# A graph-attention kernel: edge weights read from PSUM, and gathers issued in pairs behind VectorE's instructions

## The chip, the cores and the metric

The kernel runs on one core of a Trainium2 chip. The metric is the time of one execution in microseconds of the device (us). The core has TensorE (PE in the profile), VectorE (DVE), ScalarE (ACT), GpSimd (POOL) and SyncE (SP, which here only issues DMAs). They run side by side, each through its own list of instructions in order, and wait for each other by semaphores. PSUM is the memory TensorE writes to; it is divided into banks of 512 fp32 numbers per partition.

## What is computed

One layer of graph attention over 12,500 nodes of 256 features and 200,000 edges sorted by their target node `dst`:

```
h = relu(layernorm(x))
q, k, v = h @ Wq, h @ Wk, h @ Wv            # 8 heads of 32
logits = sum_d(q[dst] * k[src]) / sqrt(32)  # per edge and head
expv = exp(logits - segment_max(logits, dst)[dst])
agg = segment_sum(expv / segment_sum(expv, dst)[dst] * v[src], dst)
h2 = gelu(agg + h @ Wskip)
out = x + layernorm(h + h2)
```

Biases, gamma and beta are in the reference too.

## The kernel before

A first stage (to about 383 us) computes h, q, k and v for all nodes, writes them to tables in device memory (k and v together as 512 fp32 numbers a node, `kv_tab`), and plans the walk over the edges.

The walk (`walk_streams`) cuts the sorted edges into 8 streams of 25,000 edges and goes through all of them at once in 66 steps of 3 tiles (the last has 2). In a tile, each of 128 partitions holds one edge of each stream. Tile j of step c goes through these functions:

- `gather` (L1008): 8 indirect DMAs on POOL, one per stream, each fetching 128 rows of `kv_tab` into a quarter-megabyte slice of a buffer `kv`. There are 6 such buffers, so tile j of step c+2 takes the buffer of tile j of step c. `gather_next` (L1016) calls it right after the weighing that frees the buffer; all 8 are then in POOL's list.
- `spread` (L1042): TensorE multiplies a one-hot matrix with a window of q, which gives q of each edge's target in PSUM (`ps_qe`).
- `times` (L1054), twice per tile (streams 0 to 3 and 4 to 7): VectorE multiplies `ps_qe` with k, in place in `kv`.
- `total` (L1061): VectorE sums over the 32 numbers of a head: the logits L.
- `turn` (L1070): TensorE transposes L into PSUM (`ps_x`), edges along the free dimension. With tile 0, ScalarE then copies the last maximum of the step before into column 0 (L1077).

Once all 3 tiles of a step are turned, `maxima` (L1080) runs two scans and a subtraction on VectorE, `exponent` the exponential on ScalarE, `turn_back` (L1095) three transpositions on TensorE back to edges on partitions, in `ps_x`, and `weights` (L1104) a ScalarE copy from there to `w` in SBUF. `carried` (L1111) copies the weights of tiles 1 and 2 into `vw`. `weigh` (L1120) multiplies, on VectorE, the weights (each broadcast over 32 numbers) with v from `kv` into `vw` (L1124), and for tile 0 also L1129. `add_up` then sums `vw` over the edges of a node with TensorE, by one-hot matrices.

`ps_x` is a new tile of one bank in each step, from a pool with one buffer.

Beside the walk, nodes whose sums are complete are finished in pairs of 128-node blocks (`Pair`, L810), one stage a step: first `turn`, `divisors`, `divide`, `skip` (8 matmuls, L864), `add` (VectorE, L869) and `gelu`, in the next step `stats` (L875 and after), `root` (ScalarE, with a table load), `factors`, `scale` (L892, L896) and `store`. Pairs begin at step 10; not every step has one.

The order of each engine's work is written out by hand: `keep` (L779) ties each instruction to the one before it on the same engine. VectorE's order in the main loop, for step c, is: `times(c, 2)` twice, `total(c, 2)`, `weigh(c-1, 2)`, `maxima(c)`, `stats`, `times(c+1, 0)` twice, `total(c+1, 0)`, `weigh(c, 0)`, `divisors`, `divide`, `factors`, `add`, `times(c+1, 1)` twice, `total(c+1, 1)`, `weigh(c, 1)`, `scale`. TensorE's has `spread`, `turn`, the sums, `hot_n` and `hot_e` (one-hot matrices) and a pair's `turn` and `skip` between them.

The functions that the change touches, with the line numbers of the profile:

Of the kernel before, what the change touches and what calls it, by code (L numbers as in the profile page):

```python
# [28 lines left out]
F32 = mybir.dt.float32  # L29
# [5 lines left out]
OP = mybir.AluOpType  # L35
AX = mybir.AxisListType
SP = mybir.EngineType.SP
PSUM = bass.MemoryType.PSUM
DRAM = bass.MemoryType.DRAM

P = 128
HEADS = 8
# [4 lines left out]
S = 8  # L47
K = 3
# [712 lines left out]
def walk_streams(tc, N, HID, NST, KL, many, ident, idx, d0_row, slot_row, near, near_n, e_tab, pen_tab, h_tab,  # L761
# [174 lines left out]
    with ExitStack() as es:  # L936
# [35 lines left out]
        def tiles_of(c):  # L972
            return KL if c == NST - 1 else K


        step = [dict() for _ in range(NST + 3)]

        def where(s):
# [26 lines left out]
                q = at_byte(q_b, node, w // 2, KV).rearrange("n (k d) -> (n k) d", k=2)  # L1005
                keep(nc.sync.dma_start(qw[at:at + w, i, :].bitcast(U8), q))

        def gather(c, j):  # L1008
            t = gath.tile([P, S, KV], F32, name="kv")
            for s in range(S):  # L1010
                nc.gpsimd.indirect_dma_start(  # L1011
                    out=t[:, s, :], out_offset=None, in_=kv_tab[:, :],
                    in_offset=bass.IndirectOffsetOnAxis(ap=idx[:, s, j, c:c + 1], axis=0))
            step[c].setdefault("kv", []).append(t)

        def gather_next(c, j):  # L1016

            if c + 2 < NST and j < tiles_of(c + 2):
                gather(c + 2, j)

        def hot_e(c, i):

# [31 lines left out]
        def times(c, j, half):  # L1054

            g = step[c]
            k = g["kv"][j][:, 4 * half:4 * half + 4, :HID].rearrange("p (a b) d -> p a b d", a=2)
            keep(nc.vector.tensor_tensor(k, g["qe", half].rearrange("p b a d -> p a b d"), k,  # L1058
                                         op=OP.mult))

        def total(c, j):  # L1061
            g = step[c]
            if j == 0:
                g["L"] = work.tile([P, K, SH], F32, name="L")
            keep(nc.vector.tensor_reduce(g["L"][:, j, :].rearrange("p (s h) -> p s h", s=S),  # L1065
                                         g["kv"][j][:, :, :HID].rearrange(
                                             "p s (h d) -> p s h d", h=HEADS),
                                         AX.X, OP.add))

        def turn(c, j):  # L1070

            g = step[c]
            if j == 0:
                g["xt"] = xt_ps.tile([P, 512], F32, name="ps_x")
            keep(nc.tensor.transpose(g["xt"][:SH, j * P:(j + 1) * P], g["L"][:, j, :], ident))  # L1075
            if j == 0:
                keep(nc.scalar.copy(g["xt"][:SH, 0:1],  # L1077
                                    low0 if c == 0 else step[c - 1]["M"][:, CH - 1:]))

        def maxima(c):  # L1080
            g = step[c]
            n = tiles_of(c) * P
            X, R, pen = g["xt"][:SH, :n], g["xt"][SH:, :n], g["pen"]
            M = g["M"] = work.tile([SH, CH], F32, name="M")[:, :n]
            W = g["W"] = work.tile([SH, CH], F32, name="W", bufs=1)[:, :n]
            keep(nc.vector.tensor_tensor_scan(R, pen[:SH, :n], X, -BIG, op0=OP.add, op1=OP.max))  # L1086
            keep(nc.vector.tensor_tensor_scan(mirrored(M, 0, n), mirrored(pen[SH:, :], 1, n),  # L1087
                                              mirrored(R, 0, n), -BIG, op0=OP.add, op1=OP.max))
            keep(nc.vector.tensor_tensor(W, X, M, op=OP.subtract))

        def exponent(c):
            W = step[c]["W"]
            keep(nc.scalar.activation(W, W, AF.Exp))

        def turn_back(c):  # L1095
            g = step[c]

            n = tiles_of(c)
            ps = g["xt"][:, :K * SH].rearrange("p (k n) -> p k n", k=K)
            for j in range(n):  # L1100
                keep(nc.tensor.transpose(ps[:, j, :], g["W"][:, j * P:(j + 1) * P],
                                         ident[:SH, :SH]))

        def weights(c):  # L1104
            g = step[c]
            n = tiles_of(c)
            ps = g["xt"][:, :K * SH].rearrange("p (k n) -> p k n", k=K)
            g["w"] = work.tile([P, K, SH], F32, name="w", bufs=1)
            keep(nc.scalar.copy(g["w"][:, :n, :], ps[:, :n, :]))  # L1109

        def carried(c):  # L1111

            g = step[c]
            g["vw"] = [work.tile([P, S, SUMS], F32, name="vw", bufs=K) for _ in range(K)]
            keep(nc.scalar.copy(wden[c % 2][0:1], g["kv"][0][0:1, :, HID - HEADS:HID]))
            for j in range(1, tiles_of(c)):
                keep(nc.scalar.copy(g["vw"][j][:, :, :HEADS],
                                    g["w"][:, j, :].rearrange("p (s h) -> p s h", s=S)))

        def weigh(c, j):  # L1120
            g = step[c]
            t = g["vw"][j]
            wj = g["w"][:, j, :].rearrange("p (s h) -> p s h", s=S)
            keep(nc.vector.tensor_tensor(  # L1124
                t[:, :, HEADS:].rearrange("p s (h d) -> p s h d", h=HEADS),
                wj[:, :, :, None].to_broadcast([P, S, HEADS, D]),
                g["kv"][j][:, :, HID:].rearrange("p s (h d) -> p s h d", h=HEADS), op=OP.mult))
            if j == 0:
                keep(nc.vector.tensor_tensor(t[:, :, :HEADS], wj, wden[c % 2], op=OP.mult))  # L1129
# [100 lines left out]
        for c in range(NST - 1):  # L1230
# [9 lines left out]
                windows(c + 2)  # L1240
            for half in range(2):
                times(c, K - 1, half)
                spread(c + 1, 0, half)
            total(c, K - 1)
            turn(c, K - 1)
            if c:
                weigh(c - 1, K - 1)
                gather_next(c - 1, K - 1)
            maxima(c)
            if before:  # L1250
                before.stats()
            if c:
# [3 lines left out]
            turn_back(c)  # L1256
            if c:
                add_up_results(c - 1, 1)
            weights(c)
# [82 lines left out]
            pair.divisors()  # L1342
            pair.divide()
        turn_back(c)
        weights(c)
        carried(c)
        if before:
            before.root()
# [406 lines left out]
```

## Time and profile before

| | |
|---|---|
| three runs | 2769.89, 2772.73, 2779.48 us (median 2772.73) |
| the profiled execution | 2777.54 us; its span, from the first to the last instruction, 2775.8 us |
| busy, share of the span | DVE 74%, POOL 73%, PE 61%, ACT 38% |
| gathers (L1011) | 1576, 1827.4 us busy, from 383.7 to 2688.8 us |
| weighing (L1124) | 197 instructions, 449.7 us |
| `times` (L1058) | 394 instructions, 475.8 us |
| DMA share of 16 engines | 0.75 from 432 to 816 us, 0.80 from 816 to 2690 us |

A row of groups in the profile reads: line, engine, operation, output<-input, count | busy us, mean ns of one | idle time of the engine just before them, and what ended most of it. A row of the timeline reads: start, duration, engine, line, operation, output<-input, count, and in brackets the idle time before it and who ended it; where there is no bracket there was none. "issue" is idle time in which the engine waited for nothing that the profile shows. A gather's row shows POOL's part, the making of the transfer's descriptors; the transfer itself runs on the DMA engines after that.

### The profile page before, as it was taken

The numbers are of one execution on the slowest core, as the hardware profiler recorded it, in microseconds if no ns is written. First come the engines' busy times: TensorE is split into PE (matmuls) and PEld (weight loads), VectorE is DVE, ScalarE is ACT, GpSimd is POOL, SyncE is SP. The second block draws the span as 40 slices with busy tenths as digits, with TensorE's granted clock in tenths as the row PEclk, the third lists the DMA queues.
The fourth block names the chain that finished last, engine by engine and source line by source line (L and its number), as shares of the span: only waits on it lengthen the run. The fifth ranks groups of instructions, "written<-read, shape, count | busy, mean of one in ns | idle before, by whom it ended". The sixth has DMA issues, their size and how long they took to land.

```text
span 2775.8 us, 28386 instructions
## 1 busy us (share of the span) xinstructions
PE 1689.7 (61%) x7374; PEld 860.0 (31%) x7374; DVE 2048.7 (74%) x2416; ACT 1059.1 (38%) x2425; POOL 2028.5 (73%) x1767
## 2 busy tenths in 40 slices
PE   6779864444456656656565656566566556566554
PEld 3445432222223323322232333233233223233222
DVE  8766936666667777777777877777778778777674
ACT  3333322222234434444434434444444344344343
POOL 5634657777777777777777777777777777777760
PEclk9999975555566656566555655565666566565556
DMA  8667777777777887887788788787878878878853
GB/s 294 243 248 282 272 258 225 223 219 221 219 241 223 251 249 239 249 254 235 236 246 247 239 248 247 239 245 241 250 234 245 248 231 245 259 224 250 256 173 95
DMA packets 309574, 662.25 MB, mean 239 GB/s; under 512 B 53217, under 2 KB 193000, under 8 KB 304404
## 3 DMA queue, kind: packets, MB, share of 16 engines
q0 software_dynamic: 128768, 423.23, 50.8%
q1 hardware_dynamic: 179746, 236.30, 25.4%
q8 instruction: 61, 1.00, 0.2%
q14 instruction: 113, 0.93, 0.1%
q10 hardware_dynamic: 886, 0.79, 0.1%
HBM read 539.04 MB, written 121.07 MB: 238 GB/s over the span
## 4 chain that ended last, share of the span: by engine, by line
POOL 40%; DMA 16%; issue 16%; DVE 15%; PE 9%; ACT 2%; SPq 0%; DVEq 0%; another core or an unknown queue 0%; POOLq 0%; ACTq 0%
POOL kv L1011 39%; DMA kv<-kv_tab,idx 13%; DVE kv L1058 4%; PE ps_kv L258 4%; DVE vw L1124 3%; DVE L L1065 2%; PE ps_q L264 2%; PE ps_a L864 2%; DMA out_dram<-sums 1%; DVE M L1087 1%; DVE ps_x L1086 1%; DVE st L879 1%; ACT L885 1%; DMA sums<-table 0%; DVE sums L875 0%
## 5 line engine op out<-in xcount | busy, mean ns | idle before, releaser
L1011 POOL DMA_INDIRECT kv<-kv_tab,idx x1576 | 1827.4, 1160 | 482.2 <-issue 446.3
L1058 DVE TENSOR_TENSOR kv<-ps_qe,kv 128x1024 f32<-128x1024 f32 x394 | 475.8, 1219 | 442.9 <-DMA kv<-kv_tab,idx 433.6
L1049 PE MATMUL ps_qe<-qw,to_e 64*128 64x256 f32 (+1 forms) x1576 | 343.7, 416 | 542.2 <-DVE kv L1058 538.7
L1049 PEld LDWEIGHTS ps_qe<-qw,to_e 64*128 64x128 f32 (+1 forms) x1576 | 239.9, 265 | 760.1 <-DVE kv L1058 717.6
L1124 DVE TENSOR_TENSOR vw<-w,kv 128x2048 f32<-128x2048 f32 x197 | 449.7, 2283 | 10.7 <-ACT w L1109 10.7
L1065 DVE TENSOR_REDUCE L<-kv 128x64 f32<-128x2048 f32 x197 | 450.4, 2286 | 6.9 <-DVE kv L1058 0.2
L1148 PE MATMUL ps_a<-vw,to_n 128*32 128x264 f32 (+1 forms) x2344 | 318.1, 579 | 119.6 <-DVE vw L1124 117.2
L1028 ACT ACTIVATE to_e<-ps_hot,ones 128x384 fp32r<-128x384 f32 x396 | 213.3, 578 | 402.6 <-PE ps_hot L1026 392.7
L1160 ACT COPY sums_w<-ps_a 128x264 f32<-128x264 f32 x130 | 49.3, 380 | 804.7 <-PE ps_a L1148 552.0
L258 PE MATMUL ps_kv<-w_kv,hT 128*128 128x512 f32 x392 | 200.4, 633 | 23.2 <-ACT hT L141 22.0
L1026 PE MATMUL ps_hot<-et,near 48*128 48x384 bf16 x396 | 156.3, 457 | 67.2 <-ACT to_e L1028 62.2
L864 PE MATMUL ps_a<-w_s,hT 128*128 128x256 f32 x368 | 168.0, 636 | 44.8 <-ACT hT L850 43.4
L1148 PEld LDWEIGHTS ps_a<-vw,to_n 128*32 128x32 f32 (+1 forms) x2344 | 108.8, 155 | 279.1 <-DVE vw L1124 153.4
L270 POOL TENSOR_TENSOR qp<-qp 128x256 fp32r<-128x256 f32 x98 | 90.1, 921 | 139.0 <-ACT qp L269 138.7
L1148 PE MATMUL ps_hot<-vw,to_n 128*64 128x264 f32 x808 | 190.1, 639 | 0.0
L1075 PE MATMUL ps_x<-ident,L 128*64 128x128 f32 x197 | 78.0, 396 | 169.3 <-DVE L L1065 168.9
L1039 ACT ACTIVATE to_n<-ps_hot,ones 128x384 f32<-128x384 f32 x197 | 105.1, 579 | 124.6 <-PE ps_hot L1037 120.1
L1166 ACT COPY kv<-ps_a 1x264 f32<-1x264 f32 x388 | 143.2, 369 | 6.4
L864 PEld LDWEIGHTS ps_a<-w_s,hT 128*128 128x128 f32 x368 | 113.9, 324 | 89.2 <-ACT hT L850 64.7
L970 ACT ACT_TABLE_LOAD x102 | 130.9, 1283 | 1.9
L869 DVE TENSOR_TENSOR sums<-ps_a,sums 128x512 f32<-128x512 f32 x46 | 31.8, 691 | 134.6 <-PE ps_a L864 134.6
L264 PE MATMUL ps_q<-w_q,hT 128*128 128x256 f32 x392 | 106.4, 395 | 36.7 <-DVE qp L268 36.7
(267 smaller groups left out, 1925.6 us busy)
## 6 DMA issues: line engine op xcount, KB each, us to landing
qw<-q_pc SPq DMA_DIRECT2D x264, 128.0 KB
kv<-kv_tab,idx POOLq DMA_INDIRECT x1576
kv_tab<-kvo SPq DMA_DIRECT2D x16, 1280.0 KB
q_pc<-qp SPq DMA_DIRECT2D x16, 1280.0 KB
qw<-q_pc SPq DMA_DIRECT2D x264, 64.0 KB
table<-sums_w SPq DMA_DIRECT2D x264, 61.9 KB
pen<-pen_tab SPq DMA_DIRECT2D x66, 192.5 KB
sums<-table SPq DMA_DIRECT2D x92, 132.0 KB
```

What stands on the lines that cost most here:

```text
L258: ins = nc.tensor.matmul(ps_kv, hT[:, c, :], w_kv[:, c, :], start=c == 0, stop=c == KC - 1)
L264: ins = nc.tensor.matmul(ps_q, hT[:, c, :], w_q[:, c, :], start=c == 0, stop=c == KC - 1)
L864: self.keep(nc.tensor.matmul(self.ps[:, b, :], self.hT[:, b, c, :], w_s[:, c, :], start=False, stop=c == KC - 1, skip_group_check=True))
L1011: nc.gpsimd.indirect_dma_start(out=t[:, s, :], out_offset=None, in_=kv_tab[:, :], in_offset=bass.IndirectOffsetOnAxis(ap=idx[:, s, j, c:c ...
L1026: keep(nc.tensor.matmul(ps[:, :CH], near[:, i * P:(i + 1) * P], step[c]["et"], start=True, stop=True))
L1028: keep(nc.scalar.activation(step[c]["to_e"][:, i, :], ps[:, :CH], AF.Relu, scale=-1.0, bias=ones))
L1049: keep(nc.tensor.matmul(ps[:, b, a, :], g["to_e"][at:at + w, i, j * P:(j + 1) * P], g["qw"][at:at + w, i, :], start=True, stop=True))
L1058: keep(nc.vector.tensor_tensor(k, g["qe", half].rearrange("p b a d -> p a b d"), k, op=OP.mult))
L1065: keep(nc.vector.tensor_reduce(g["L"][:, j, :].rearrange("p (s h) -> p s h", s=S), g["kv"][j][:, :, :HID].rearrange("p s (h d) -> p s h d" ...
L1124: keep(nc.vector.tensor_tensor(t[:, :, HEADS:].rearrange("p s (h d) -> p s h d", h=HEADS), wj[:, :, :, None].to_broadcast([P, S, HEADS, D] ...
L1148: keep(nc.tensor.matmul(ps[at:at + w, :], g["to_n"][:, j, i * P + at:i * P + at + w], g["vw"][j][:, s, :], start=j == 0, stop=j == tiles_o ...
L1166: keep(nc.scalar.copy(step[c + 1]["kv"][0][0:1, s, HID - HEADS:], ps[at:at + 1, :]))
```

## The change

`ps_x` becomes one tile for the whole walk, `turned`, 512 columns in one bank: columns 0 to 383 hold the transposed logits as before, and `turn_back` writes the weights of tile 0 into columns 0 to 63, of tile 1 into 384 to 447, of tile 2 into 448 to 511. The function `weights` and its copy to SBUF are gone: `carried` and `weigh` read the weights from PSUM.

The 8 gathers of a tile are given out as 4 pairs. Pair 0 stands where all 8 stood, right after the weighing that frees the buffer. Pairs 1, 2 and 3 stand behind later instructions of VectorE, and the first gather of each of these pairs waits, by a semaphore, for the VectorE instruction written last before it (`latest[DVE]`). All gathers of the main loop are tied into POOL's written order by `keep`. For the buffer of tile 0 the pairs follow `weigh(c, 0)`, the two `times(c+1, 1)` and `total(c+1, 1)`; for tile 1 `weigh(c, 1)`, and in the next step the two `times` and the `total` of tile 2; for tile 2 `weigh(c-1, 2)`, the last instruction of `maxima(c)`, and the two `times(c+1, 0)`. The first two steps' 48 gathers come without waits, as before.

```
+        turned = xt_ps.tile([P, CH + 2 * SH], F32, name="ps_x")
...
-        def gather(c, j):
-            t = gath.tile([P, S, KV], F32, name="kv")
-            for s in range(S):
-                nc.gpsimd.indirect_dma_start(
+        def gather(c, j, slots=range(S), behind=None):
+            if slots[0] == 0:
+                step[c].setdefault("kv", []).append(gath.tile([P, S, KV], F32, name="kv"))
+            t = step[c]["kv"][j]
+            for s in slots:
+                ins = keep(nc.gpsimd.indirect_dma_start(
                     out=t[:, s, :], out_offset=None, in_=kv_tab[:, :],
-                    in_offset=bass.IndirectOffsetOnAxis(ap=idx[:, s, j, c:c + 1], axis=0))
-            step[c].setdefault("kv", []).append(t)
-        def gather_next(c, j):
-            if c + 2 < NST and j < tiles_of(c + 2):
-                gather(c + 2, j)
+                    in_offset=bass.IndirectOffsetOnAxis(ap=idx[:, s, j, c:c + 1], axis=0)))
+                if behind and s == slots[0]:
+                    tc.add_manual_dep(ins.ins, behind, mybir.DependencyInfo(
+                        mybir.DependencyClass.Sync, mybir.DependencyReason.DATA), reason="pace")
+        def gather_next(c, j, part):
+            if 0 <= c < NST - 2 and j < tiles_of(c + 2):
+                gather(c + 2, j, range(2 * part, 2 * part + 2), latest[DVE] if part else None)
...
         def turn(c, j):
             g = step[c]
+            keep(nc.tensor.transpose(turned[:SH, j * P:(j + 1) * P], g["L"][:, j, :], ident))
             if j == 0:
-                g["xt"] = xt_ps.tile([P, 512], F32, name="ps_x")
-            keep(nc.tensor.transpose(g["xt"][:SH, j * P:(j + 1) * P], g["L"][:, j, :], ident))
-            if j == 0:
-                keep(nc.scalar.copy(g["xt"][:SH, 0:1],
+                keep(nc.scalar.copy(turned[:SH, 0:1],
                                     low0 if c == 0 else step[c - 1]["M"][:, CH - 1:]))
...
-            X, R, pen = g["xt"][:SH, :n], g["xt"][SH:, :n], g["pen"]
+            X, R, pen = turned[:SH, :n], turned[SH:, :n], g["pen"]
...
+        def weight(j):
+            at = CH + (j - 1) * SH if j else 0
+            return turned[:, at:at + SH].rearrange("p (s h) -> p s h", s=S)
         def turn_back(c):
-            ps = g["xt"][:, :K * SH].rearrange("p (k n) -> p k n", k=K)
...
-        def weights(c):
-            g["w"] = work.tile([P, K, SH], F32, name="w", bufs=1)
-            keep(nc.scalar.copy(g["w"][:, :n, :], ps[:, :n, :]))
...
-                keep(nc.scalar.copy(g["vw"][j][:, :, :HEADS],
-                                    g["w"][:, j, :].rearrange("p (s h) -> p s h", s=S)))
+                keep(nc.scalar.copy(g["vw"][j][:, :, :HEADS], weight(j)))
         def weigh(c, j):
-            wj = g["w"][:, j, :].rearrange("p (s h) -> p s h", s=S)
+            wj = weight(j)
...
                 times(c, K - 1, half)
+                gather_next(c - 1, 1, 1 + half)
                 spread(c + 1, 0, half)
             total(c, K - 1)
+            gather_next(c - 1, 1, 3)
             turn(c, K - 1)
             if c:
                 weigh(c - 1, K - 1)
-                gather_next(c - 1, K - 1)
+                gather_next(c - 1, K - 1, 0)
             maxima(c)
+            gather_next(c - 1, K - 1, 1)
...
                 times(c + 1, 0, half)
+                gather_next(c - 1, K - 1, 2 + half)
                 spread(c + 1, 1, half)
             total(c + 1, 0)
             weigh(c, 0)
-            gather_next(c, 0)
+            gather_next(c, 0, 0)
...
                 times(c + 1, 1, half)
+                gather_next(c, 0, 1 + half)
...
             total(c + 1, 1)
+            gather_next(c, 0, 3)
             turn(c + 1, 1)
             weigh(c, 1)
-            gather_next(c, 1)
+            gather_next(c, 1, 0)
```

More of the change, by code (lines that the diff above doesn't have):

```diff
@@ L37 @@
 SP = mybir.EngineType.SP
+DVE = mybir.EngineType.DVE
 PSUM = bass.MemoryType.PSUM
@@ L1093, in exponent @@
             keep(nc.scalar.activation(W, W, AF.Exp))
+        def weight(j):
+            at = CH + (j - 1) * SH if j else 0
+            return turned[:, at:at + SH].rearrange("p (s h) -> p s h", s=S)
         def turn_back(c):
-            g = step[c]
-            n = tiles_of(c)
-            ps = g["xt"][:, :K * SH].rearrange("p (k n) -> p k n", k=K)
-            for j in range(n):
-                keep(nc.tensor.transpose(ps[:, j, :], g["W"][:, j * P:(j + 1) * P],
-                                         ident[:SH, :SH]))
-        def weights(c):
-            g = step[c]
-            n = tiles_of(c)
-            ps = g["xt"][:, :K * SH].rearrange("p (k n) -> p k n", k=K)
-            g["w"] = work.tile([P, K, SH], F32, name="w", bufs=1)
-            keep(nc.scalar.copy(g["w"][:, :n, :], ps[:, :n, :]))
+            for j in range(tiles_of(c)):
+                keep(nc.tensor.transpose(weight(j).rearrange("p s h -> p (s h)"),
+                                         step[c]["W"][:, j * P:(j + 1) * P], ident[:SH, :SH]))
         def carried(c):
@@ L1258, in walk_streams @@
                 add_up_results(c - 1, 1)
-            weights(c)
             if c:
@@ L1344, in walk_streams @@
         turn_back(c)
-        weights(c)
         carried(c)
```

## The prediction

> **What bounds the kernel now.** I read the page's busy shares first, then the costliest groups, then the timeline of two steps, then the list of waits.
>
> ```profile
> PE 1689.7 (61%) x7374; PEld 860.0 (31%) x7374; DVE 2048.7 (74%) x2416; ACT 1059.1 (38%) x2425; POOL 2028.5 (73%) x1767
> ...
> L1011 POOL DMA_INDIRECT kv<-kv_tab,idx x1576 | 1827.4, 1160 | 482.2 <-issue 446.3
> L1058 DVE TENSOR_TENSOR kv<-ps_qe,kv 128x1024 f32<-128x1024 f32 x394 | 475.8, 1219 | 442.9 <-DMA kv<-kv_tab,idx 433.6
> ```
>
> No engine looks full. But the gathers (L1011) fill POOL: 1827.4 us busy, and 446.3 of the 482.2 us of idle time in front of them is "issue", 0.30 us a gather. From the first gather at 383.7 us to the last at 2688.8 us, 2306 us, 1827.4 + 482.2 = 2309.6 are accounted for (0.30 x 1576 = 473 of the idle is the issue): POOL never waits for a buffer, and VectorE waits 433.6 us for gathered rows. POOL sets the pace. Why its mean is 1160 ns, when the median of that line is 947, is seen in the timeline:
>
> ```profile
> 1507.21 0.95 POOL L1011 DMA_INDIRECT kv<-kv_tab,idx  x1 [0.30 <-issue]
> 1508.46 0.95 POOL L1011 DMA_INDIRECT kv<-kv_tab,idx  x1 [0.30 <-issue]
> 1508.61 2.28 DVE L1124 TENSOR_TENSOR vw<-w,kv 128x2048 f32<-128x2048 f32 x1
> ...
> 1509.71 2.00 POOL L1011 DMA_INDIRECT kv<-kv_tab,idx  x1 [0.30 <-issue]
> ...
> 1514.93 1.23 DVE L1058 TENSOR_TENSOR kv<-ps_qe,kv 128x1024 f32<-128x1024 f32 x1
> ...
> 1515.07 0.95 POOL L1011 DMA_INDIRECT kv<-kv_tab,idx  x1 [0.30 <-issue]
> ```
>
> A gather that starts while the weighing (L1124, `vw<-w,kv`, two inputs in SBUF) runs ends 0.82 us after the weighing does; one under `times` (L1058, one input in PSUM, one in SBUF) takes its 0.95 us. I set all 1576 gather rows against VectorE's rows, by what VectorE runs 0.13 us after the gather's start. Weighing: 205 gathers, 193 stretched, 309.7 us in all. L875 (two SBUF inputs): 44 of 44, 23.9 us. `times`: 350 gathers, 1 stretched. L1065: 356, none. VectorE idle: 446, 2 by hundredths. So a VectorE tensor-tensor with both inputs in SBUF holds a gather; one with an input in PSUM does not.
>
> The Trainium skill speaks against this change here: "SBUF — State Buffer", section "Who interferes with whom", says that a tensor_tensor with two SBUF inputs contends with GpSimd's reads only, and infers that descriptor generation, which needs the write interface, is not stalled by it. By that rule moving the weights to PSUM frees nothing, and the sum below would keep its added waits and lose its gain. The 193 of 205 rows above say otherwise for this gather, and I follow them.
>
> **Steps by class.** From one L1129 row (once per step) to the next, with VectorE's waits before L1058 taken out, the 65 steps are:
> - 11 early, no pair: mean 34.93 us, of them VectorE's own chain 23.48
> - 34 with a pair's `add` and another's `scale`: 35.77, chain 31.63
> - 10 with `add` only: 33.27, chain 29.13
> - 9 with `scale` only: 36.13, chain 25.27
> - the last: 35.2, left as it is
>
> POOL's own need is 24 gathers x 1.25 = 30.0 us, plus stalls 309.7/64 = 4.8: 34.8. That is why classes with such different chains last about the same.
>
> **The change, part by part.**
>
> 1. *Weighing reads PSUM.* Removes 4.8 us of POOL time a step; POOL's need falls to 30.0, about 30.2 with L875's stalls (0.67 us long; at most 0.4 a step). The weighing's own time: L869 (PSUM and SBUF) takes 0.691, L875 of the same shape from SBUF 0.673, so +0.02 each, 3 a step; nothing. The copy L1109 (0.32 us, ScalarE, 38% busy) goes, and `carried`'s copies read PSUM; ScalarE's idle hides both; uncovered they would be 0.7 us a step, and a wait of the weighing for L1109 was seen once, in the last step.
>
> 2. *The first tile's `turn` now waits for the weighing.* The weights of tile 0 lie in columns 0 to 63, over which `turn(c+1, 0)` writes. Before, it ran beside the weighing. Behind it in TensorE's queue stand a pair's `turn` and `skip`, `hot_e` and `spread`; behind its ScalarE copy (L1077) stand the table load, the root and the copy of hT; and VectorE's `add` waits for all of it:
>
> ```profile
> 1522.38 2.28 DVE L1124 TENSOR_TENSOR vw<-w,kv 128x2048 f32<-128x2048 f32 x1
> ...
> 1522.62 0.40 PE L1075 MATMUL ps_x<-ident,L 128*64 128x128 f32 x1 [0.27 <-DVE L L1065]
> ...
> 1523.05 0.16 ACT L1077 COPY ps_x<-M 64x1 f32<-64x1 f32 x1
> 1523.22 1.28 ACT L885 ACT_TABLE_LOAD   x1
> ...
> 1524.72 0.57 ACT L850 COPY hT<-ps_hot 128x512 f32<-128x512 f32 x1
> ...
> 1525.34 3.49 PE L864 MATMUL ps_a<-w_s,hT 128*128 128x256 f32 x8 [0.94 <-ACT hT L850]
> ...
> 1528.87 0.69 DVE L869 TENSOR_TENSOR sums<-ps_a,sums 128x512 f32<-128x512 f32 x1 [2.89 <-PE ps_a L864]
> ```
>
> From the turn's start to `add` is 6.25 us. After, it starts when L1129 ends (1524.81): `add` at about 1531.1 where it was at 1528.9. VectorE has 1.17 us of other work there, so its wait grows from 2.9 to about 5.1: +2.1 us in the 44 steps with an `add`. Nothing else can fill it: VectorE's order is fixed.
>
> 3. *One bank for everything.* `turn(c, 2)` is written just ahead of `weigh(c-1, 2)`, and `turn(c+1, 1)` ahead of `weigh(c, 1)`: TensorE writes columns of the bank that VectorE reads others of. Before, the weighing started 0.09 us ahead of the recorded end of L1065. If the two are kept in order, VectorE waits for the transposition. The first step, with no weighing, shows that price:
>
> ```profile
> 419.13 2.29 DVE L1065 TENSOR_REDUCE L<-kv 128x64 f32<-128x2048 f32 x1
> ...
> 421.47 0.42 PE L1075 MATMUL ps_x<-ident,L 128*64 128x128 f32 x1 [1.10 <-DVE L L1065]
> 421.99 0.96 DVE L1086 TENSOR_TENSOR_SCAN ps_x<-pen,ps_x 64x384 f32<-64x384 f32 x1 [0.57 <-PE ps_x L1075]
> ```
>
> 0.57 + 0.09 = 0.66 us, twice a step: 1.3. The bounds are 0 (different columns, no order) and 1.3, unless TensorE is late (its `spread` in front takes 1.22, inside L1065's 2.29). In this kernel's trace no two engines are seen in one bank at once, so I take 1.3 and keep 0. The skill's "PSUM — Partial Sum Buffer", section on bank collisions, says two engines must not be in one bank and quadrant at a time, reads included; that speaks for the 1.3, and no run here shows it.
>
> 4. *Gathers in pairs behind VectorE's instructions.* Nothing is added; each pair of a tile may start only when a named VectorE instruction has ended, at 12 places a step. Only gathers are queued behind a waiting gather; `times` waits for them. SP's queue is not touched. A pair takes POOL 2.5 us; from the first `times` of tile 2 to the second of the next tile 0 seven marks come within 13 us, so POOL is up to 5 us late there; it catches up and idles 5 to 6 us in VectorE's long wait for `skip`, and is some 4 us late after it. The shortest way from a mark to its use is from L1065 of tile 1 to the second half of the next step's tile 0: weighing 2.9 with its wait, scale 1.75, two `times` 2.4, L1065 2.3, weighing 2.9, L1086 to L1089 2.5, stats 1.7, `times` 1.2: 17.7 us. Landing takes, over the 147 waits of `times` longer than 0.3 us, 2.3 to 6.5 us from the gather's end, median 3.15. 17.7 - 4 - 3.2 leaves 10 us: the marks cost nothing where VectorE's chain is the longer. In the early steps POOL is the longer, always behind, and the marks are past.
>
> **The sum**, against the profiled execution's 2777.5 us (span 2775.8):
> - early: POOL's 30.2 for 34.93, 11 steps: -52
> - `add` and `scale`: 31.63 + 1.3 + 2.1 = 35.0 for 35.77, 34 steps: -26
> - `add` only: 29.13 + 3.4 = 32.5 for 33.27, 10 steps: -8
> - `scale` only: chain 26.6, POOL 30; it can fall behind by some of its 10 us of slack, so between, 28.5, for 36.13, 9 steps: -69
>
> Together -155: 2623 us. The bound moves from POOL to VectorE in two steps of three, so most of POOL's 310 us is not seen. The profiled execution lies 4.8 us above the median of the runs shown.
>
> **Rivals.**
> - *No order within the bank.* Then 1.3 us a step go back in the 53 later steps: -69, about 2555. For it: the columns are disjoint. Against: the accesses share one bank.
> - *The gain is eaten in part.* Data moves faster: the DMA share of 0.75 to 0.80 of these steps rises to about 0.87, landings spread, and TensorE's waits are longer than the rows, say 1 to 2 us a step in 53: 2675 to 2730. For it: landings already reach 6.5 us.
> - *The hold stays*, and the change does not do what it says: POOL needs 34.8 as now, and the chain of 35.0 takes turns with it: by the steps where one waits for the other, 0 to +30, 2775 to 2810. Against it: 1 of 350 under `times`, which has the same operands in the same order.
> - *Slower through the marks.* Place: the pair behind L1065 of tile 1. If landing passes 3.2 + 10 = 13 us, VectorE waits for it in every step, 1 us for each us; past 16 us (3 us x 53 steps) the whole gain is gone, and at 18 us it is 2623 + 5 x 53 = 2890. Against it: the longest landing now is 6.5.
>
> **How the numbers follow.** Forecast (2590 to 2665) 0.52; no order in the bank 0.17; eaten in part 0.16; hold stays 0.07; slower through the marks or another wait of that size 0.08. The range takes in the first three and leaves out the last two: 2550 to 2730. Three runs lie within 0.35% of each other, so 0.3% is about what can be told from no change: faster 0.85, same 0.05 (most of "hold stays"), slower 0.10.
>
> **What would show it.** Gathers beside L1124's successor at 0.95 us: step 1 right. L869's wait for TensorE near 5 us in place of 2.9: step 2. A wait of 0.6 us for `ps_x` before two weighings a step: step 3. POOL idle behind VectorE after the weighing of tile 0, and `times` waiting for rows in the early steps only: step 4. Early steps at 30 us, steps with an `add` at 33 to 35. I am wrong if gathers stay stretched, or if `times` still waits for rows in steps with an `add`.

## The result, and the profile after

| | before | after |
|---|---|---|
| median of the runs | 2775.77 us (2769.89 to 2779.48, 4 runs) | 2624.99 us (2617.95 to 2625.08, 4 runs) |
| profiled execution, its span | 2777.54, 2775.8 us | 2617.95, 2616.2 us |

The ratio is 0.9452, 95% interval [0.9427, 0.9477]: 5.5% faster, 2 us from the forecast of 2623 us. In the later runs, made on four chips (numbers 15, 10, 12 and 8; the number of this table's chip is not known), the kernel before takes 2941 to 2988 us, and the changed kernel, on the chip where it was run again, is 12% *slower* than the kernel before; that is the larger part of the experiments below. "On record" means the executions of this table, "later" those of the experiments.

The page of the changed kernel has these rows (its lines have moved: the gather is L1017, `times` L1066, the weighing L1123):

```profile
PE 1659.4 (63%) x7374; PEld 837.1 (32%) x7374; DVE 2063.0 (79%) x2416; ACT 1037.6 (40%) x2359; POOL 1717.7 (66%) x1767
...
L1017 POOL DMA_INDIRECT kv<-kv_tab,idx x1576 | 1517.3, 963 | 623.3 <-issue 360.8
L1066 DVE TENSOR_TENSOR kv<-ps_qe,kv 128x1024 f32<-128x1024 f32 x394 | 464.9, 1216 | 79.7 <-DMA kv<-kv_tab,idx 78.4
L1123 DVE TENSOR_TENSOR vw<-ps_x,kv 128x2048 f32<-128x2048 f32 x197 | 451.0, 2289 | 88.0 <-PE ps_x L1081 68.0
```

The gathers fell from 1827.4 to 1517.3 us, 963 ns a piece. VectorE waits 78.4 us for gathered rows where it waited 433.6, and waits 88.0 us ahead of the weighing, where it waited 10.7. The timeline of one step and a half shows the steps of the prediction one after another:

```profile
1501.40 2.28 DVE L1123 TENSOR_TENSOR vw<-ps_x,kv 128x2048 f32<-128x2048 f32 x1
1501.94 0.95 POOL L1017 DMA_INDIRECT kv<-kv_tab,idx  x1 [0.30 <-issue]
1503.19 0.95 POOL L1017 DMA_INDIRECT kv<-kv_tab,idx  x1 [0.30 <-issue]
...
1503.86 0.42 PE L1081 MATMUL ps_x<-ident,L 128*64 128x128 f32 x1 [2.65 <-DVE vw L1128]
1504.38 0.16 ACT L1083 COPY ps_x<-M 64x1 f32<-64x1 f32 x1 [2.55 <-PE ps_x L1081]
...
1506.16 0.17 DVE L889 RECIPROCAL rstd<-rstd 128x2 f32<-128x2 f32 x1 [2.35 <-ACT rstd L886]
...
1511.56 2.29 DVE L1123 TENSOR_TENSOR vw<-ps_x,kv 128x2048 f32<-128x2048 f32 x1 [0.52 <-PE ps_x L1081]
...
1537.83 0.69 DVE L870 TENSOR_TENSOR sums<-ps_a,sums 128x512 f32<-128x512 f32 x1 [3.81 <-PE ps_a L865]
...
1539.92 0.95 POOL L1017 DMA_INDIRECT kv<-kv_tab,idx  x1 [1.92 <-DVE kv L1066]
```

Two gathers run beside a weighing in 0.95 us each (before, a held one took 1.89 to 3.06). The turn of tile 0 (L1081) starts when the weighing's last instruction ends; `factors` (L889) waits behind it for ScalarE's root; the weighing at 1511.56 waits 0.52 us for a transposition into its own bank; `add` (L870) waits 3.81 us for TensorE; and GpSimd waits for a mark, the `times` at L1066. The list of waits gives the totals (engine, tile and line; who released it; us in total, times, longest):

```profile
DVE sums L870 <- PE ps_a L865: 184.7, 45, 4.7
POOL kv L1017 <- DVE kv L1066: 183.3, 142, 5.8
...
DVE kv L1066 <- DMA kv<-kv_tab,idx: 78.4, 28, 11.0
...
DVE vw L1123 <- PE ps_x L1081: 68.0, 129, 0.6
...
DVE rstd L889 <- ACT rstd L886: 62.6, 45, 2.6
...
DVE vw L1123 <- ACT vw L1117: 20.0, 18, 7.2
```

By class of step, from the end of one weighing of tile 0 to the next:

| steps | before | forecast | after | sum of the difference |
|---|---|---|---|---|
| 11 early | 34.93 | 30.2 | 30.44 | -49 |
| 34 `add` and `scale` | 35.77 | 35.0 | 34.79 | -33 |
| 10 `add` only | 33.27 | 32.5 | 31.98 | -13 |
| 9 `scale` only | 36.13 | 28.5 | 29.01 | -64 |

With 0.7 us less in the last step that is -160, the whole difference of the spans (-159.6).

### The profile page after: what moved, and what is told of

It is laid out like the page before. It is cut to its first block, busy times and chain, and to the rows that moved or that the text cites. A ratio compares the mean times of both kernels' runs of the same rounds, so it can differ in the third digit from the quotient of the medians.

```text
span 2616.2 us, 28875 instructions
## 1 busy us (share of the span) xinstructions
PE 1659.4 (63%) x7374; PEld 837.1 (32%) x7374; DVE 2063.0 (79%) x2416; ACT 1037.6 (40%) x2359; POOL 1717.7 (66%) x1767
## 4 chain that ended last, share of the span: by engine, by line
DVE 23%; POOL 22%; DMA 22%; issue 20%; PE 9%; ACT 2%; SPq 1%; DVEq 0%; POOLq 0%; another core or an unknown queue 0%; ACTq 0%
POOL kv L1017 21%; DMA kv<-kv_tab,idx 17%; DVE kv L1066 5%; DVE vw L1123 5%; DVE L L1073 5%; PE ps_kv L259 4%; PE ps_q L265 2%; DMA out_dram<-sums 1%; DVE ps_x L1092 1%; DVE M L1093 1%; PE ps_x L1081 1%; DMA sums<-table 1%; DMA qw<-q_pc 1%; PE ps_hot L1147 1%; PE ps_a L865 1%
## 5 line engine op out<-in xcount | busy, mean ns | idle before, releaser
L1017 POOL DMA_INDIRECT kv<-kv_tab,idx x1576 | 1517.3, 963 | 623.3 <-issue 360.8
L1066 DVE TENSOR_TENSOR kv<-ps_qe,kv 128x1024 f32<-128x1024 f32 x394 | 464.9, 1216 | 79.7 <-DMA kv<-kv_tab,idx 78.4
L1123 DVE TENSOR_TENSOR vw<-ps_x,kv 128x2048 f32<-128x2048 f32 x197 | 451.0, 2289 | 88.0 <-PE ps_x L1081 68.0
L1057 PE MATMUL ps_qe<-qw,to_e 64*128 64x256 f32 (+1 forms) x1576 | 331.7, 406 | 232.9 <-issue 108.6
L1081 PE MATMUL ps_x<-ident,L 128*64 128x128 f32 x197 | 78.5, 399 | 297.9 <-DVE L L1073 154.7
L1147 PEld LDWEIGHTS ps_a<-vw,to_n 128*32 128x32 f32 (+1 forms) x2344 | 95.3, 145 | 331.4 <-DVE vw L1123 222.0
L870 DVE TENSOR_TENSOR sums<-ps_a,sums 128x512 f32<-128x512 f32 x46 | 31.8, 691 | 184.7 <-PE ps_a L865 184.7
L1081 PEld LDWEIGHTS ps_x<-ident,L 128*64 128x64 f32 x197 | 24.7, 125 | 412.2 <-DVE vw L1128 219.3
```

The costliest lines, as they stand in the source:

```text
L1017: ins = keep(nc.gpsimd.indirect_dma_start(out=t[:, s, :], out_offset=None, in_=kv_tab[:, :], in_offset=bass.IndirectOffsetOnAxis(ap=idx[:, ...
L1057: keep(nc.tensor.matmul(ps[:, b, a, :], g["to_e"][at:at + w, i, j * P:(j + 1) * P], g["qw"][at:at + w, i, :], start=True, stop=True))
L1123: keep(nc.vector.tensor_tensor(t[:, :, HEADS:].rearrange("p s (h d) -> p s h d", h=HEADS), wj[:, :, :, None].to_broadcast([P, S, HEADS, D] ...
L1147: keep(nc.tensor.matmul(ps[at:at + w, :], g["to_n"][:, j, i * P + at:i * P + at + w], g["vw"][j][:, s, :], start=j == 0, stop=j == tiles_o ...
```

## The experiments

Theory at the outset: the gain is the hold that is gone; what is left above 30 us a step is VectorE's chain, lengthened by the turn that waits (step 2) and the bank's order (step 3). The rival: the marks, not the hold, make the gain, or take part of it. The first four kernels were each priced for a chip on which the kernel before takes 2773 us.

**marks_only.** The kernel before with the gathers given out in pairs behind VectorE's instructions; the weights stay in SBUF.

```
-                gather_next(c - 1, K - 1)
+                gather_next(c - 1, K - 1, 0)
             maxima(c)
+            gather_next(c - 1, K - 1, 1)
...
```

> Weights copied to SBUF as before, gathers in pairs behind VectorE's instructions. My theory: the weighing still holds some 200 gathers for 310 us, POOL needs 34.8 us a step, and the pairs now wait for marks too: 2775 to 2810 us, no gain. Rival (the marks bring the gain): 2640 to 2700, with fewer gathers stretched because the marks move them out of the weighing.

Measured: 2963.6 us beside 2941.43 of the kernel before, ratio 1.0066 [1.0026, 1.0107]. 180 of 185 gathers under the weighing are stretched, by 292.7 us in all: the marks alone do not take the hold away, and bring no gain there.

**psum_only**, and again in the next group as **psum_only_2.** The changed kernel without the marks: all eight gathers of a tile behind the weighing.

```
-                gather(c + 2, j, range(2 * part, 2 * part + 2), latest[DVE] if part else None)
+                gather(c + 2, j)
...
-                gather_next(c - 1, 1, 1 + half)
...
-            gather_next(c - 1, 1, 3)
```

> Weights read from PSUM, all 8 gathers of a tile right behind the weighing, without marks. My theory (the hold is the gain, the marks cost nothing): 2625 us, within 10 of the changed kernel, no gather stretched under the weighing, the early steps 30.4 us, steps with an add and a scale 34.8. Rival (the marks are a part of the gain, since they spread the transfers): 2650 to 2700, with waits of times for rows in the steps with an add.

> The changed kernel without the marks: all eight gathers of a tile behind the weighing, as in the kernel before, weights still read from PSUM. If the marks cost and bring nothing (step 4 of the prediction), it is within 1 per cent of the changed kernel, 2600 to 2650 where the kernel before is at 2773. Rival: gathers given out eight at a time land earlier but bunch up transfers and delay others: over 1 per cent slower. If the chip of the group before is not special, 1.0955 of the kernel before again.

Measured: 3228.94 us, ratio 1.0955 [1.0888, 1.1022]; again 3228.82, 1.0958 [1.0857, 1.1059]. The hold is gone (0 of 93 gathers under the weighing stretched), and the kernel is 10% slower than the kernel before. Neither theory allowed for that.

**skip_early**, again as **skip_early_2; weigh_first; both.** Three orders of the changed kernel: the pair's `skip` chain and `root` ahead of the turn of tile 0, and `hot_n` behind it; the weighing of tile 1 ahead of the turn that it shares the bank with; and both.

```
+            if pair:                       # skip_early
+                pair.turn(); pair.divisors(); pair.divide(); pair.skip()
+            if before:
+                before.root()
+            turn(c + 1, 0)
             for j in range(K):
                 hot_n(c, j)
-            turn(c + 1, 0)
...
-            turn(c + 1, 1)                 # weigh_first
             weigh(c, 1)
             gather_next(c, 1, 0)
+            turn(c + 1, 1)
```

> The changed kernel, with a pair's turn, skip and root written ahead of turn(c+1, 0), and hot_n behind it, so that TensorE does them beside the weighing. My theory (the wait of add for skip, 4.1 + 1.1 us of 34.8, is what VectorE's chain is too long by): that wait falls to 1 us or less, the steps fall to POOL's 30.0 to 30.8, 2460 to 2500 us in all. Rival (TensorE is full there, and the wait moves to hot_n, hot_e and spread behind skip): 2560 to 2630, with VectorE waiting for ps_qe or ps_x instead.

> The changed kernel with only the skip chain and root() ahead of turn(c+1,0) and hot_n. The add's wait falls from 4.1 to 1.0 or less, the factors' wait from 1.1 to 0.1, as in the group before (there 1.00 and 0.10). Steps with a pair to add and to scale fall from 34.8 by 3 to 4: 2616 - 34*3.3 - 10*1.2 = about 2490, 2460 to 2560, where the kernel before is at 2773. If the chip of the group before is not special, 1.074 of the kernel before again, as there.

> The changed kernel, with weigh(c, 1) written ahead of turn(c+1, 1), so that only the transposition waits. My theory (0.57 us of wait and 0.09 of overlap, once a step): in the 53 later steps 0.6 us less each, 2593 us; in the early steps nothing. Rival (the bank is not what the weighing waits for): 2625.

> The changed kernel with the skip chain of the pair and root() ahead of turn(c+1,0) and hot_n, and the weighing ahead of turn(c+1,1). If the 4.1 us wait of VectorE's add (44 steps) and the 2.35 us wait of factors (43 steps) are what is left above GpSimd's 30.0 us per step, then steps fall to 30.3 to 31.5 in all classes: 2616 - 34*3.8 - 10*1.2 = about 2475 us, 2440 to 2520. Rival: the weighing's wait for TensorE or for a landing takes their place, 2560 to 2620. By theory A these numbers hold only where the kernel before is at 2773; where it is at 2940, 3050 to 3300.

Measured: skip_early 3163.97 us, ratio 1.0737 [1.0672, 1.0803], and again 3159.9, 1.072 [1.0619, 1.0822]; weigh_first 3310.02, 1.1236 [1.1163, 1.1308]; both 3165.86, 1.0746 [1.0647, 1.0844]. All are slower than the kernel before, so either the edits or the place cost it.

**after_again.** So the changed kernel itself was run there, with nothing edited.

> The changed kernel itself, nothing edited, as the yardstick for the others of this group. In the group before, the kernel before took 2941 us instead of 2773, and four variants of the change took 2964 to 3310; in their traces instructions that wait for TensorE alone (the copy of the sums at L1159, the weighing at L1123) start 7 to 12 us after the matmul they wait for, while GpSimd issues gathers back to back. Theory A (that chip delays such releases, more so the less the gathers are held): if the kernel before is at about 2773 here, this one is at 2618 to 2630, ratio 0.945; if it is at about 2940 here, this one is slower than it, 2980 to 3230. Rival B (the edits of that group cost it, whatever the chip): ratio 0.945 in both cases.

Measured: 3309.59 us beside 2953.81, ratio 1.1234 [1.1128, 1.134]. The edits are not to blame, rival B falls: the change that gains 5.5% on record loses 12% here. Against this yardstick of 3310 us the orders can be read: skip_early is 150 us faster, psum_only 81 us faster, weigh_first the same. Where the time lies, the page says in two rows:

```profile
L1017 POOL DMA_INDIRECT kv<-kv_tab,idx x1576 | 1511.3, 959 | 1317.6 <-issue 418.8
L1123 DVE TENSOR_TENSOR vw<-ps_x,kv 128x2048 f32<-128x2048 f32 x197 | 451.4, 2291 | 800.5 <-ACT vw L1117 477.5
```

No gather is held (1511.3 us), `times` waits for rows in 7 places only, and the weighing, of the same 2.29 us, now has 800.5 us of idle time ahead of it where it had 88.0. Against the execution on record the wait ahead of the weighing grew by 712 us; 54 us of VectorE's wait for rows went; and 664 us is what the steps became longer. That one wait is the whole loss. (Beside the kernel before in its own later execution, before_again below, it is 535 us longer, for a span that is 366 us longer.) What it is, the timeline of one step shows:

```profile
1495.90 1.11 PE L1147 MATMUL ps_a<-vw,to_n 128*32 128x264 f32 x8 [2.38 <-issue]
...
1496.94 2.75 PE L1147 MATMUL ps_hot<-vw,to_n 128*64 128x264 f32 x12
...
1504.55 0.38 ACT L1159 COPY sums_w<-ps_a 128x264 f32<-128x264 f32 x1 [17.81 <-remote]
...
1507.67 0.95 POOL L1017 DMA_INDIRECT kv<-kv_tab,idx  x1 [0.30 <-issue]
1511.80 0.38 ACT L1159 COPY sums_w<-ps_hot 128x264 f32<-128x264 f32 x1 [5.00 <-remote]
...
1512.86 0.38 ACT L1159 COPY sums_w<-ps_a 128x264 f32<-128x264 f32 x1
...
1513.93 0.24 ACT L1115 COPY wden<-kv 1x64 f32<-1x64 f32 x1
1514.19 0.33 ACT L1117 COPY vw<-ps_x 128x64 f32<-128x64 f32 x2
1514.56 2.29 DVE L1123 TENSOR_TENSOR vw<-ps_x,kv 128x2048 f32<-128x2048 f32 x1 [9.87 <-ACT vw L1117]
1517.12 0.95 POOL L1017 DMA_INDIRECT kv<-kv_tab,idx  x1 [8.49 <-DVE den L840]
```

The same place in the execution on record:

```profile
1523.92 2.91 PE L1147 MATMUL ps_hot<-vw,to_n 128*64 128x264 f32 x12
...
1526.87 0.38 ACT L1159 COPY sums_w<-ps_hot 128x264 f32<-128x264 f32 x1 [0.57 <-PE ps_hot L1147]
...
1528.79 0.38 ACT L1159 COPY sums_w<-ps_a 128x264 f32<-128x264 f32 x1 [0.88 <-PE ps_a L1147]
...
1530.49 2.29 DVE L1123 TENSOR_TENSOR vw<-ps_x,kv 128x2048 f32<-128x2048 f32 x1 [0.51 <-ACT vw L1117]
```

ScalarE's copy of the sums in `ps_hot` waits for one thing, their twelve matmuls. On record it starts with their end (1523.92 + 2.91 = 1526.83, start 1526.87); later, 12.1 us after it (1496.94 + 2.75 = 1499.69, start 1511.80), with nothing in the record that released it ("remote" is a releaser that the trace doesn't have). Of the 12.1 us, 5.00 are its own wait: the copy ahead of it in ScalarE's queue, which waits for the eight matmuls of `ps_a`, is late too (they end at 1497.01, it starts at 1504.55; the stores that it also waits for had landed 18 us earlier). Behind both in ScalarE's queue stand the row carried from step to step and the weights' copies L1117, and the weighing of tile 0 waits for those. From 900 us on, the median lag of the `ps_hot` copy behind its matmuls is 0.05 us in the two executions on record and 11.8 us here, and the weighing of tile 2, which waits for TensorE's transposition alone, is over 2 us late in 14 of 54 steps. Of the 53 starts of these two that come over 2 us late, 52 lie 2.5 to 3.5 us (to the nearest half) after the end of a gather behind which GpSimd pauses, as if they had waited until the last gather in flight had landed. But the copy of `ps_a` ahead of them is over 2 us late in 33 steps, and none of these lies there. Nor is it always the same instruction: in skip_early the `ps_hot` copy's median lag is 0.05 us again, and the late ones are the weighing of tile 2 (52 of 54 steps) and the second copy of `ps_a` (49 of 54).

What differs beside that: the first stage takes as long as on record (the first gather starts at 383.7 us on record and at 385.7 in before_again), the kernel before has a granted clock of 0.654 and 0.660, and the traces of the later executions hold 23 to 27 thousand semaphore events where the two on record hold 60 thousand. Who ended a wait is inferred from these events, so the releasers named in the later rows are less sure than their times.

**after_copy, before_again, one_window.** Three questions: does undoing the read of PSUM alone bring the time back; how does the kernel before look there; and is it SyncE's issue of transfers that disturbs?

```
+        def weights(c):                                  # after_copy
+            w = step[c]["w"] = work.tile([P, K, SH], F32, name="w", bufs=1)
+            keep(nc.scalar.copy(w[:, 0, :], ...))
+            keep(nc.scalar.copy(w[:, 1:1 + n, :], ...))
...
-            wj = weight(j)
+            wj = g["w"][:, j, :].rearrange("p (s h) -> p s h", s=S)
```

```
-            for s, node in enumerate(nodes(c)):          # one_window
-                ...
-                keep(nc.sync.dma_start(qw[at:at + w, i, :].bitcast(U8), q))
+            q = q_pc[:QT * P // 2, :].rearrange("n (k d) -> (n k) d", k=2)
+            keep(nc.sync.dma_start(qw.bitcast(U8), q.rearrange("(i p) d -> p i d", p=P).bitcast(U8)))
```

> The changed kernel with one part undone: ScalarE copies the weights to SBUF again and the weighing reads them there; marks, the bank and the rest of the order stay. GpSimd's gathers under the weighing are then held again (about 185 of 200, 1.5 us each, 290 us in all). Where the kernel before is at 2773, theory: 2760 to 2800, the gain gone. Where it is at about 2950 and the changed kernel at 3310 (the group before), theory A (what is lost there comes from GpSimd issuing gathers with nothing that holds it): 2930 to 3000, that is faster than the changed kernel by 10 per cent. Rival (the shared bank or its order costs it): over 3150.

> The kernel before, for its trace beside those of this group. Theory A: its gathers are held (193 of 205 under the weighing), pauses of the gathers' packets are under 60 and under 250 us in all, and the copies of the sums (L1160) start within 1 us of their matmuls in most steps. Rival (this condition slows every kernel alike): pauses as many as in the changed kernel.

> The changed kernel with SyncE's eight loads of the query windows per step (L1009, 0.5 to 1 us of issue each) made one load of as many bytes, from fixed rows: it leaves out that each block gets its own query rows. In the group before, no packet of a gather moved for 4 to 8 us at a time while GpSimd went on issuing (130 pauses, 731 us in the changed kernel; 34 of 3 us, 90 us, in the execution on record), mostly while SyncE issued L1009, L1169 or L904. Theory C (SyncE's issue beside GpSimd's makes the pauses): those at L1009 go, about a third; 3310 falls to 3100 to 3230. Rival (they only coincide): 3280 to 3330. Where the kernel before is at 2773, both say 2600 to 2630.

Measured: after_copy 2971.12 us beside 2948.03, ratio 1.0059 [1.0014, 1.0105]; one_window 3276.12, 1.1098 [1.105, 1.1146]; before_again one run, 2944.95. The one edit of after_copy takes back nearly all of the 12%, and the hold is back with it, as two rows of its timeline show (a gather of 3.05 us where the weighing starts just ahead of it):

```profile
1485.47 2.28 DVE L1131 TENSOR_TENSOR vw<-w,kv 128x2048 f32<-128x2048 f32 x1
1485.53 3.05 POOL L1017 DMA_INDIRECT kv<-kv_tab,idx  x1 [0.30 <-issue]
```

184 of 189 gathers under its weighing are stretched, 304.8 us in all. The marks and the one tile for all steps, which after_copy keeps, together cost 0.6% there. It undoes step 3 along with the read: its weighings of tiles 1 and 2 start 0.08 us ahead of the recorded end of `total` again, as in the kernel before, where those of after_again start 0.52 us behind it. Against that as the cause speaks weigh_first, which frees one of the two waits and is no faster. So the rival of the marks falls, and that of the bank's order has little left. The kernel before, in its groups by line:

```profile
L1011 POOL DMA_INDIRECT kv<-kv_tab,idx x1576 | 1773.6, 1125 | 694.5 <-issue 480.5 <-DVE vw L1124 93.8 <-ACT ps_x L1077 78.9
L1124 DVE TENSOR_TENSOR vw<-w,kv 128x2048 f32<-128x2048 f32 x197 | 449.9, 2284 | 265.4 <-ACT kv L1166 188.8 <-issue 57.6 <-ACT w L1109 10.2
```

It is disturbed too, its weighing waits 265.4 us where on record it waits 10.7, but the copy of `ps_hot` lags over 2 us in 5 of 56 steps only. Late releases are in it from the start, where all 48 gathers of the first two steps are issued in one unbroken run. The `times` of 417.13 waits only for the four matmuls that end at 409.41, and starts 7.7 us after them:

```profile
408.61 0.80 PE L1049 MATMUL ps_qe<-qw,to_e 64*128 64x256 f32 x4 [2.61 <-issue]
...
417.13 1.22 DVE L1058 TENSOR_TENSOR kv<-ps_qe,kv 128x1024 f32<-128x1024 f32 x1 [6.38 <-remote]
```

The same place in the execution on record, with the same unbroken run beside it, has no wait:

```profile
405.06 0.80 PE L1049 MATMUL ps_qe<-qw,to_e 64*128 64x256 f32 x4 [1.28 <-DVE kv L1058]
...
407.13 1.15 DVE L1058 TENSOR_TENSOR kv<-ps_qe,kv 128x1024 f32<-128x1024 f32 x1
```

The first weighing of tile 0 ends 31 us later than on record (463.3 for 432.3 us). Until then no weighing has run, no gather is marked and the weights are copied to SBUF: the late releases need neither the weighing's read of PSUM nor the marks.

Stretches of over 1.5 us in which no packet of the gathers' queue moves, though a gather has been issued, are 24 (39 us in all) in the kernel before on record, 34 (90 us) in the changed one on record, 53 (234 us) in before_again, 50 (208 us) in after_copy, 127 (716 us) in after_again, 130 (652 us) in one_window. But one_window, which makes one of eight of SyncE's issues a step (and leaves out that each block gets its own query rows), gains 1%, far from the 80 to 210 us of theory C: SyncE's issue of those loads is at most a small part of it.

**paced.** A small clear on GpSimd behind each gather, so that the gathers come slower without a hold.

```
                         mybir.DependencyClass.Sync, mybir.DependencyReason.DATA), reason="pace")
+                keep(nc.gpsimd.memset(pause, 0.0))
```

> The changed kernel, weights still read from PSUM, with a small clear of an idle tile on GpSimd behind each gather (128x64, estimated 0.1 to 0.2 us from the 0.20 us of a 128x128 clear), so that 24 gathers take about 34 to 36 us per step, as when 4 or 5 of them are held, but without any hold. In the groups before, the kernel before was at 2950, the changed kernel at 3310 and the one that copies the weights back at 2971. Theory P (there the unbroken pitch of the gathers, 1.25 us, is what hurts): 2950 to 3080. Rival W (it is the weighing's read of PSUM or the waits around it, whatever the pitch): 3250 to 3400. Where the kernel before is at 2773, both say 2740 to 2830, since GpSimd's need is back at 34 to 36 us.

Measured: 3392.72 us beside 2988.06, ratio 1.1332 [1.1263, 1.1401]. The groups by line:

```profile
L1018 POOL DMA_INDIRECT kv<-kv_tab,idx x1576 | 1532.0, 972 | 1117.1 <-DVE kv L1068 282.7 <-DVE vw L1125 263.6 <-issue 240.5
...
L1024 POOL MEMSET pause<- 128x64 f32 x1576 | 275.0, 175 | 5.2 <-remote 4.1 <-issue 0.9
```

The clear takes its 0.175 us, but fits into the gap of 0.30 us that stands before each gather anyway. In unbroken stretches the pitch is 1.33 us (1.28 without the clears, 1.42 to 1.43 where the weighing holds gathers), so 24 gathers need 32 us and not the 34 to 36 of the expectation. A pitch 4% longer brought no gain; whether the longer one of a held kernel would, or the break of 1.5 us at each weighing, was not tried by it. Theory P is not borne out, and not quite dead. The wait ahead of the weighing is 884.8 us there, though the `ps_hot` copy's median lag is 0.20 us.

**What stays open.** Shown: in the later executions the loss of the changed kernel is the wait ahead of the weighing; it comes with the weights' move to PSUM. Of the 356 us that the changed kernel is behind there, leaving the marks out gives back 81 (psum_only_2), the other order of the turns 150 (skip_early_2), one load in place of SyncE's eight some 33, copying the weights back nearly all. Not shown: why releases by TensorE come 8 to 12 us late there and not on record, and whether the read of PSUM or the hold's absence makes them so many in the changed kernel; after_copy changes both at once. The first step of before_again, where releases are late beside an unbroken run of gathers and before any weighing, speaks for the hold's absence; paced speaks against a pitch 4% longer as the remedy. Also open is whether chip or time makes the difference: the times of the kernel before on the four later chips agree within 1.6%, and lie 6 to 8% above the time on record. And no variant was run where the change gains: that the 5.5% on record come from the hold, and not in part from the marks, is read from the rows and the classes of step, not from an experiment.

## Why the prediction was right, and where it was not

The number and its range hold for the execution on record. They do not hold for the later ones, and no rival named what happened there. That the median lies within 2 us of the sum is partly luck: by class of step the profiled execution is off the forecast by +3, -7, -5 and +5 us, which partly cancel, and it lies 7 us below the median.

1. **Weighing reads PSUM: right.** Under the weighing 193 of 205 gathers were stretched, 309.7 us; after, 1 of 352. In after_copy, with the copy back, 184 of 189, 304.8 us. The gathers fell by 310.1 us in the page's rows. The weighing takes 2.289 us for 2.283. The few that were not held have a reason too: every held gather began 0.04 us or more after the weighing's start, every one not held at most 0.02 us after it (in marks_only and after_copy together, 0.028 and 0.025). The inference of the Trainium skill that was set against this ("SBUF — State Buffer", "Who interferes with whom": descriptor generation is not stalled) is refuted by these rows for this gather. The rule behind it, that such a tensor_tensor contends with GpSimd's reads, is not: the gather has `idx` among its inputs, though no run here varies that.

2. **The turn that waits: its sum was right, its place only in part.** Forecast was `add` waiting 5.1 us for 2.9. In steps with `add` and `scale` the wait grew from 3.14 to 4.09, and `factors`, which had not waited, waits 1.11 ahead of it: 5.2 together. With `add` only it grew from 2.42 to 4.14, 1.7 for the 2.1 forecast. The `factors` wait stands behind the same ScalarE copy (L1083) that the prediction named, yet it was not followed to `root` and L889. skip_early moves both chains ahead of the turn. Its list of waits in the second group, beside that of after_again:

```profile
DVE sums L870 <- PE ps_a L865: 33.3, 29, 2.1
...
DVE rstd L889 <- ACT rstd L886: 12.3, 4, 4.2
```

```profile
DVE sums L870 <- PE ps_a L865: 187.5, 45, 4.7
DVE rstd L889 <- ACT rstd L886: 65.0, 43, 2.6
```

Of the 207 us that these two waits lost, 150 are seen in the time. So the price of step 2 is real, and it was a matter of where the turn is written. On record nothing was run with that order.

3. **One bank: right.** The weighings of tiles 1 and 2 wait 0.51 us each, 0.60 with the 0.09 by which they had started early; forecast 0.66. In weigh_first and both, with the weighing of tile 1 ahead of the turn, it starts 0.09 early again (0.51 of wait in after_again). So TensorE's write into other columns of the bank is kept ahead of VectorE's read: both weighings wait for TensorE's semaphore, where those of the kernel before have no such wait. That wait is written in the program; whether the two could run at once without it was not tried. The rival "no order within the bank" falls. Freed, it gave nothing there: weigh_first takes as long as the changed kernel.

4. **The marks cost nothing: right on record, as far as it shows.** GpSimd idles 140 us behind L1066, 3.2 us in each of the 44 steps with an `add` (forecast 5 to 6), and `times` waits for rows 28 times, in the early steps. The gathers now end a median of 16 us before the first `times` of their tile, not 6. Later it is wrong: psum_only, without marks, is 81 us faster than the changed kernel.

5. **`scale` only: nearly the number, for a wrong reason.** Forecast was 28.5 because GpSimd falls behind by its slack. GpSimd is not what these steps wait for: `times` waits for no rows in them. The chain of 25.27 became 29.0 by `factors` waiting 2.35, the two bank waits and a few tenths for ScalarE. The forecast's term for `factors` was nothing.

6. **Slower.** The rival of 0.08 had a mechanism (rows landing too late for `times`) and a price (16 us a step of landing). The later slowdown has another: TensorE's releases, late at ScalarE and at VectorE, priced at nothing, because on record the weighing's only wait for ScalarE was seen once. The prediction asked what is queued behind the turn; it did not ask what stands ahead of the weighing in ScalarE's queue, and what a late start there would cost once GpSimd no longer sets the pace. That the result might hang on where or when it is measured was in no case of the prediction.

## What to carry to other kernels

A DMA that an engine issues can be held by what another engine reads; to see it, set every issue against what the other engine runs at that moment, and look for durations that end together. When the slowest engine is freed, follow everything that stands ahead of the instruction that sets the pace next, in every queue, because each of those waits now costs its full length. And measure a change that removes slack on more than one chip and occasion: this one took 5.5% off the time on record and added 12% later.

## What the runs showed of the hardware that was not expected

- A copy on ScalarE that waits only for TensorE started 0.05 us after its matmuls on record, and a median of 11.8 us after them in after_again (of which a median of 4.6 us was ScalarE idle just ahead of it), in the same program, at a granted clock of 0.67 and 0.63.
- In the kernel before, `times` starts 7.7 us after the matmuls that it waits for beside an unbroken run of gathers (before_again, 417.13 us), and without a wait on record.
- Gathers are issued at 0.95 us while their transfers stand still: 4 to 8 us at a time in after_again, 2 to 3 us in the execution on record.
- VectorE's L876, both inputs in SBUF, still stretches 40 of 40 gathers (15.8 us), and L854, of the same kind, 23 of 38 (7.1 us), while L1123 with one input in PSUM stretches 1 of 352. The 15 others of L854 began up to 0.03 us ahead of it, or with 0.13 us of it left: a gather that is first is not held.
- A clear of 0.175 us between two gathers is nearly hidden in the 0.30 us that GpSimd idles before each: the pitch grows by 0.05 us.
